# Cross attention: products over heads and keys packed into five chunks of 128 rows instead of eight of 77

## The chip, the core and the metric

The kernel runs on one core of a Trainium2 chip. The metric is the device time of one execution in microseconds (us). A core has TensorE (PE in the profile; PEld is its loading of stationary operands), VectorE (DVE), ScalarE (ACT), GpSimd (POOL) and SyncE (SP), each with its own queue of instructions in program order, and 16 DMA engines that they share. Matmuls read on-chip memory (SBUF, 128 rows called partitions) and write PSUM, from which DVE and ACT copy.

## The reference

Sixteen batches, each with 256 queries of width 256 and 77 keys of context width 192; eight heads of width 256; all float32.

```python
Q = (img_embed @ Wq).reshape(B, -1, H, D).transpose(0, 2, 1, 3)
K = (sent_embed @ Wk).reshape(B, -1, H, D).transpose(0, 2, 1, 3)
V = (sent_embed @ Wv).reshape(B, -1, H, D).transpose(0, 2, 1, 3)
score = jnp.einsum('bhqd,bhkd->bhqk', Q, K) / math.sqrt(D)
score = jnp.where(mask, score, -jnp.inf)
attn = jax.nn.softmax(score, axis=-1)
ctx = jnp.einsum('bhqk,bhkd->bqhd', attn, V).reshape(B, -1, H * D)
out = ctx @ Wo + img_embed
mu = jnp.mean(out, axis=-1, keepdims=True)
var = jnp.var(out, axis=-1, keepdims=True)
return (out - mu) * jax.lax.rsqrt(var + EPS) * gamma + beta
```

## The kernel before

The products are taken in another order. Once, for each head: G = Wq Wk^T / sqrt(D) (matmuls `pg`, kept transposed in `gT`) and U = Wv Wo (`pu`, kept in `u`); the context is transposed into `cT`, whose 192 rows lie in two chunks of 96. The weights, context and mask are loaded into a pool that is released after this stage; later tiles, `a` first of all, take its memory.

The rest is done in four groups of four batches. A batch has two tiles of 128 queries, so there are eight tiles (numbered `t`) in a group and 32 in all.

- `prepare_group`, at the first tile of a group: x is transposed (`px`, copied to `xT`) and A = G c^T is formed for the four batches and eight heads: 16 outputs `pa` of two matmuls of 308 columns, copied in turn by ACT and DVE into `a`.
- `scores_and_softmax(t)`: four matmuls of 308 columns give the scores `ps` (128 queries by 8 x 77). DVE adds the mask's bias (`s`), takes the largest of each head (`top`), subtracts it; ACT takes exp (`e`); DVE sums (`den`) and inverts (`rden`); POOL multiplies (`p`).
- `prepare_batch(b)`: the product of context and U, `pv`, with the 77 keys as output rows and 8 x 256 columns: four outputs of two matmuls of 512 columns, each copied by ACT into `vw`.
- `attend(t)`, two tiles later: eight transposes of `p`, one a head (`pp`), two ACT copies to `pT`, eight matmuls that contract 77 rows each and add up in `po` (256 columns); DVE adds the residual into `xg` and takes mean and variance (`bn`, `mv`).
- `normalise_group(g)`, after a group's last `attend`: the normalisation in two DVE steps a tile (the first one, with `gam`, is issued as soon as a tile's mean is there), then one store for two tiles.

The loop calls these with the attention product two tiles behind the scores. A scheduler orders each engine's queue from that code, so pieces of neighbouring tiles interleave; nothing overtakes within an engine's queue. The pools hold two buffers each for the scores, for transposes (`ps_tr`) and for all other products (`ps_mm`).

Of the kernel before, what the change touches and what calls it, by code (L numbers as in the profile page):

```python
# [8 lines left out]
F32 = mybir.dt.float32  # L9
# [6 lines left out]
P = 128  # L16
H = 8          # heads
D = 256        # head width
EPS = 1e-05
GB = 4         # batches in a group  # L20
MASKED = 3.0e38  # taken from a masked score: any score of less than 1e31 is absorbed by it


# Per head h the products are taken in this order:
#   G_h = Wq_h Wk_h^T / sqrt(D)        U_h = Wv_h Wo_h        (once)
#   A_bh = G_h c_b^T                   VW_bh = c_b U_h        (once a batch)
#   score_bh = x_b A_bh                out_b = sum_h softmax(score_bh) VW_bh
# so neither Q, K, V nor the context of a head is ever formed.
@with_exitstack
def kernel(  # L30
# [23 lines left out]
    HK = H // 2 * S2           # score columns in one PSUM bank  # L54
    assert NCR * CR == B * S2 and NG * GB == B and DI == 2 * P and D == 2 * P

# [14 lines left out]
    bias = const.tile([P, B, S2], F32, tag="bias", name="bias")  # L71
    live = const.tile([P, B], F32, tag="live", name="live")
    gam = const.tile([P, DI], F32, tag="gam", name="gam")
    bet = const.tile([P, DI], F32, tag="bet", name="bet")
# [7 lines left out]
    def load_x(g):  # L82
        xg = xp.tile([P, GT, DI], F32, tag="xg", name=f"xg_{g}")
        nc.sync.dma_start(xg, x_rows[:, g * GT : (g + 1) * GT, :])
        xg_of[g] = xg

    evacs = [0]

# [6 lines left out]

# [1 line left out]
    with tc.tile_pool(name="wload", bufs=1) as wp, tc.tile_pool(name="wt", bufs=2) as wt:  # L97
# [53 lines left out]
        for r in range(0, NCR, 2):  # L151
# [9 lines left out]
            for lc in range(2):  # L161
# [3 lines left out]
                )  # L165

        for h in range(H):
            wvT = transposed(wv_sb, LP, h, "wvT")
            pu = ps_mm.tile([P, 2, DI], F32, tag="mm", name=f"pu_{h}")
            for lc in range(2):  # L170
                for dc in range(2):
                    nc.tensor.matmul(  # L172
                        pu[:LP, lc, :],
                        wvT[:, dc, lc * LP : (lc + 1) * LP],
                        wo_sb[:, 2 * h + dc, :],
                        start=(dc == 0),
                        stop=(dc == 1),
                    )
            evacuate(u[:, :, h, :], pu[:LP])
# [3 lines left out]
        bias_f = bias.rearrange("p b k -> p (b k)")  # L183
# [6 lines left out]

# [1 line left out]
    ap = ctx.enter_context(tc.tile_pool(name="ap", bufs=2))  # L192
# [35 lines left out]

    def prepare_batch(b):
        vw = ap.tile([S2, H, DI], F32, tag="vw", name=f"vw_{b}", bufs=3)  # L230
        for n in range(H // 2):
            pv = ps_mm.tile([P, 2 * DI], F32, tag="mm", name=f"pv_{b}_{n}")
            for lc in range(2):
                nc.tensor.matmul(  # L234
                    pv[:S2],
                    cT[:, lc, b * S2 : (b + 1) * S2],
                    u[:, lc, 2 * n : 2 * n + 2, :].rearrange("p h d -> p (h d)"),
                    start=(lc == 0),
                    stop=(lc == 1),
                )  # L240
            nc.scalar.copy(vw[:, 2 * n : 2 * n + 2, :].rearrange("p h d -> p (h d)"), pv[:S2])  # L241
        vw_of[b] = vw

    def scores_and_softmax(t):
# [3 lines left out]
        for hh in range(2):  # L248
# [26 lines left out]
        nc.vector.tensor_scalar(rden, rden, live[:, b : b + 1], None, ALU.mult)  # L275
        p = sp.tile([P, H, S2], F32, tag="p", name=f"p_{t}")
        nc.gpsimd.tensor_tensor(  # L277
            p, e, rden.unsqueeze(2).to_broadcast([P, H, S2]), ALU.mult
        )
        p_of[t] = p  # L280

    def attend(t):
        g, b, j = t // GT, t // QT, t % GT
        p = p_of.pop(t)
        pT = sp.tile([S2, H, P], F32, tag="pT", name=f"pT_{t}", bufs=2)
        for hh in range(2):
            pt = ps_tr.tile([P, 4, P], F32, tag="tr", name=f"pp_{t}_{hh}")
            for i in range(4):
                nc.tensor.transpose(pt[:S2, i, :], p[:, hh * 4 + i, :], ident)  # L289
            nc.scalar.copy(pT[:, hh * 4 : hh * 4 + 4, :], pt[:S2])  # L290
        po = ps_mm.tile([P, DI], F32, tag="mm", name=f"po_{t}")
        for h in range(H):
            nc.tensor.matmul(  # L293
                po, pT[:, h, :], vw_of[b][:, h, :], start=(h == 0), stop=(h == H - 1)
            )
        y = xg_of[g][:, j, :]
# [71 lines left out]
```

## Time and profile before

| | |
|---|---|
| median of three runs | 482.4 us (482.24 to 482.61) |
| span of the profiled execution | 480.1 us; the page gives no other time of that execution |
| busy: PE, DVE, ACT, POOL | 439.0, 210.7, 136.8, 39.6 us |
| granted TensorE clock, mean | 0.977 |
| until the first score product is done | 98.69 us |
| the two middle groups | 98.2 us each |

The span is time from the first to the last instruction. Stretches below are cut where the first score product of a group ends, since everything before it in a group (px, pa, ps) is PE work on which all engines wait. A group line of the profile gives the source line, engine, operation and tile, the shape, the count, busy time and the mean of one in ns, then the idle time before them and what ended it. A float32 matmul appears as two records, a transpose as one.

### The profile page before, as it was taken

To read this page: it belongs to the slowest core of one execution; us is meant where nothing else is said; L and a number is where in the kernel's file an instruction comes from. 1 tells how busy PE (TensorE), PEld (TensorE's weight loads), DVE (VectorE), ACT (ScalarE), POOL (GpSimd) and SP (SyncE) were. 2 spreads that over 40 slices of the span, in tenths; PEclk is the share of its full clock that TensorE was granted. 3 is DMA by queue.
4 is the path that set the end of the run, shared out by engine and by line. 5 is a ranking of instruction groups with operands and counts; after the bars stand their busy time and mean duration, and the time that the engine had idled before them with its cause. 6 is when DMAs were issued, how large, how long until landed. Compare 5 with 4: busy or idle time off the path is not lost.

```text
span 480.1 us, 4689 instructions
## 1 busy us (share of the span) xinstructions
PE 439.0 (91%) x1846; PEld 298.3 (62%) x1846; DVE 210.7 (44%) x424; ACT 136.8 (28%) x242; POOL 39.6 (8%) x38
## 2 busy tenths in 40 slices
PE   1409899999999999999999999999999999999993
PEld 1307677755765875758567766585767756658572
DVE  0031223235736433375373433844735238555364
ACT  1103422223132222251333213523132134331321
POOL 0000000012112000121111101112111011121110
PEclk9859999999999999999999999999999999999997
DMA  8993000000000000022000000130000000200002
GB/s 237 256 341 106 0 1 1 0 2 0 0 1 0 1 0 0 1 87 89 0 0 1 0 0 2 53 123 0 1 1 0 1 0 1 89 0 0 2 1 87
DMA packets 13446, 17.86 MB, mean 37 GB/s; under 512 B 480, under 2 KB 12208, under 8 KB 13232
## 3 DMA queue, kind: packets, MB, share of 16 engines
q1 hardware_dynamic: 9696, 12.95, 8.9%
q10 hardware_dynamic: 3728, 4.62, 3.3%
q8 instruction: 14, 0.23, 0.2%
q14 instruction: 8, 0.07, 0.0%
HBM read 13.37 MB, written 4.19 MB: 37 GB/s over the span
## 4 chain that ended last, share of the span: by engine, by line
PE 87%; DMA 6%; DVE 3%; ACT 2%; issue 0%; DVEq 0%; ACTq 0%
PE po L293 24%; PE pv L234 22%; PE pa L218 14%; PE ps L250 14%; PE pp L289 5%; DMA m_i<-in_mask_BxS_if_dram 5%; PE pg L142 3%; PE pu L172 3%; DMA wk_sb<-in_L_xattn_Wk_dram 2%; PE px L205 2%; DVE wkT L94 1%; ACT pT L290 1%; DVE xg L313 1%; PE p_wkT L126 0%; PE p_wvT L126 0%
## 5 line engine op out<-in xcount | busy, mean ns | idle before, releaser
L293 PE MATMUL po<-vw,pT 77*128 77x256 f32 x512 | 117.2, 382 | 1.7 <-ACT pT L290 1.7
L234 PE MATMUL pv<-u,cT 96*77 96x512 f32 x256 | 113.1, 593 | 0.1
L293 PEld LDWEIGHTS po<-vw,pT 77*128 77x128 f32 x512 | 94.6, 190 | 21.3 <-ACT pT L290 9.7
L234 PEld LDWEIGHTS pv<-u,cT 96*77 96x77 f32 x256 | 37.5, 148 | 67.0 <-issue 57.8
L250 PE MATMUL ps<-a,xT 128*128 128x308 f32 x256 | 75.8, 422 | 0.0
L277 POOL TENSOR_TENSOR p<-e,rden 128x616 f32<-128x616 f32 x32 | 38.9, 1216 | 423.1 <-DVE rden L275 236.5
L218 PE MATMUL pa<-cT,gT 96*128 96x308 f32 x256 | 67.7, 422 | 0.0
L241 ACT COPY vw<-pv 77x512 f32<-77x512 f32 x64 | 37.1, 581 | 97.8 <-PE pv L234 97.5
L297 DVE TENSOR_TENSOR xg<-po,xg 128x256 f32<-128x256 f32 x32 | 13.6, 424 | 108.8 <-PE po L293 108.7
L290 ACT COPY pT<-pp 77x512 f32<-77x512 f32 x64 | 34.1, 583 | 86.5 <-PE pp L289 86.5
L218 PEld LDWEIGHTS pa<-cT,gT 96*128 96x128 f32 x256 | 48.0, 190 | 16.6
L250 PEld LDWEIGHTS ps<-a,xT 128*128 128x128 f32 x256 | 46.5, 190 | 12.4 <-issue 0.5
L289 PEld LDWEIGHTS pp<-ident,p 128*77 128x77 f32 x256 | 30.4, 148 | 11.3 <-issue 5.3
L94 DVE COPY a<-pa 128x308 f32<-128x308 f32 x32 | 15.3, 479 | 48.1 <-PE pa L218 48.1
L272 DVE TENSOR_REDUCE den<-e 128x8 f32<-128x616 f32 x32 | 25.4, 794 | 23.5 <-ACT e L270 23.4
L142 PE MATMUL pg<-wqT,wkT 128*96 128x256 f32 x64 | 18.9, 447 | 18.2 <-DVE wkT L94 18.2
L289 PE MATMUL pp<-ident,p 128*77 128x128 f32 x256 | 33.2, 272 | 0.0
L258 DVE TENSOR_TENSOR s<-ps,bias 128x616 f32<-128x616 f32 x32 | 25.6, 799 | 10.7 <-PE ps L250 10.7
L270 ACT ACTIVATE e<-s 128x616 f32<-128x616 f32 x32 | 22.9, 717 | 23.5 <-DVE s L266 23.4
L92 ACT COPY a<-pa 128x308 f32<-128x308 f32 x32 | 13.4, 418 | 48.3 <-PE pa L218 48.3
L142 PEld LDWEIGHTS pg<-wqT,wkT 128*96 128x96 f32 x64 | 11.6, 192 | 23.5 <-DVE wkT L94 19.8
L266 DVE TENSOR_TENSOR s<-s,top 128x616 f32<-128x616 f32 x32 | 25.6, 800 | 1.0
(45 smaller groups left out, 212.8 us busy)
## 6 DMA issues: line engine op xcount, KB each, us to landing
xg<-in_x_dram SPq DMA_DIRECT2D x4, 1024.0 KB, 12.5
out_dram<-xg SPq DMA_DIRECT2D x16, 256.0 KB, 2.2
wq_sb<-in_L_xattn_Wq_dram SPq DMA_DIRECT2D x2, 1024.0 KB, 12.3
wo_sb<-in_L_xattn_Wo_dram ACTq DMA_DIRECT2D x1, 2048.0 KB, 39.0
wk_sb<-in_L_xattn_Wk_dram ACTq DMA_DIRECT2D x2, 768.0 KB, 11.3
wv_sb<-in_L_xattn_Wv_dram SPq DMA_DIRECT2D x1, 1536.0 KB, 22.1
c_sb<-in_ctx_dram ACTq DMA_DIRECT2D x1, 924.0 KB, 27.3
m_i<-in_mask_BxS_if_dram SPq DMA_DIRECT2D x1, 616.0 KB, 21.7
```

The lines of the kernel that those rows point to most:

```text
L142: nc.tensor.matmul(pg[:LP, lc, :], wkT[:, dc, lc * LP : (lc + 1) * LP], wqT[:, dc, :], start=(dc == 0), stop=(dc == 1),)
L218: nc.tensor.matmul(pa.rearrange("p b k -> p (b k)"), gT[:, lc, h, dc * P : (dc + 1) * P], cT[:, lc, g * GB * S2 : (g + 1) * GB * S2], star ...
L234: nc.tensor.matmul(pv[:S2], cT[:, lc, b * S2 : (b + 1) * S2], u[:, lc, 2 * n : 2 * n + 2, :].rearrange("p h d -> p (h d)"), start=(lc == 0 ...
L241: nc.scalar.copy(vw[:, 2 * n : 2 * n + 2, :].rearrange("p h d -> p (h d)"), pv[:S2])
L250: nc.tensor.matmul(ps[:, hh, :HK], xT_of[g][:, dc, j * P : (j + 1) * P], a_of[g][:, dc, bl, hh * 4 : hh * 4 + 4, :].rearrange("p h k -> p ...
L258: nc.vector.tensor_tensor(s.rearrange("p (a h) k -> p a h k", a=2), ps[:, :, :HK].rearrange("p a (h k) -> p a h k", k=S2), bias[:, b, :].u ...
L266: nc.vector.tensor_tensor(s, s, top.unsqueeze(2).to_broadcast([P, H, S2]), ALU.subtract)
L272: nc.vector.tensor_reduce(den, e, AX.X, ALU.add)
L277: nc.gpsimd.tensor_tensor(p, e, rden.unsqueeze(2).to_broadcast([P, H, S2]), ALU.mult)
L289: nc.tensor.transpose(pt[:S2, i, :], p[:, hh * 4 + i, :], ident)
L290: nc.scalar.copy(pT[:, hh * 4 : hh * 4 + 4, :], pt[:S2])
L293: nc.tensor.matmul(po, pT[:, h, :], vw_of[b][:, h, :], start=(h == 0), stop=(h == H - 1))
```

## The change

The rows that the last product contracts, 8 heads x 77 keys = 616, are laid out as four chunks of 128 rows (two heads with 64 keys each) and one chunk of 104 rows (the last 13 keys of all eight heads), in place of eight chunks of 77.

- `p` is written by POOL in two parts in that order, and transposed in five pieces; the fifth, `pq`, has its own PSUM tile and its own ACT copy.
- `prepare_pair` takes the place of `prepare_batch`: one product for two batches, with 2 x 64 keys as the 128 output rows. Each output is copied in four pieces of 64 rows by 256 columns, to the rows where the packed layout wants them; ACT copies the even outputs, DVE the odd ones.
- The last 13 keys are done once for all batches, before the groups: two stages of eight batches, `pr` with 104 output rows, copied to `stage`, written to DRAM (`scratch`) by eight DMAs of 104 KB a stage, and loaded back by one DMA of 832 KB as `vr`, with (head, key) as rows.
- `cM` and `cR` are copies of `cT`, made by POOL, with the first 64 and last 13 keys of the batches side by side.

```diff
+        for lc in range(2):
+            keys = cT[:, lc, :].rearrange("p (b k) -> p b k", k=S2)
+            nc.gpsimd.tensor_copy(cM[:, lc], keys[:, :, :KM])
+            nc.gpsimd.tensor_copy(cR[:, lc], keys[:, :, KM:])
...
+        for r in range(B // RB):
+            stage = wp.tile([RB * KR, H, DI], F32, tag=("c", "wq")[r], name=f"stage_{r}")
+            for n in range(H // 2):
+                pv = ps_mm.tile([P, 2 * DI], F32, tag="mm", name=f"pr_{r}_{n}")
...
+                evacuate(
...
+            for i in range(RB):
+                nc.sync.dma_start(
+                    scratch[r * RB + i].rearrange("h k d -> k h d"),
+                    stage[i * KR : (i + 1) * KR],
+                )
+            nc.sync.dma_start(
+                vr[:, r * RB : (r + 1) * RB, :],
+                scratch[r * RB : (r + 1) * RB].rearrange("b h k d -> (h k) b d"),
+            )
...
-                    pv[:S2],
-                    cT[:, lc, b * S2 : (b + 1) * S2],
+                    pv.rearrange("p h d -> p (h d)"),
+                    cM[:, lc, b : b + 2, :].rearrange("p b k -> p (b k)"),
...
-            nc.scalar.copy(vw[:, 2 * n : 2 * n + 2, :].rearrange("p h d -> p (h d)"), pv[:S2])
-        vw_of[b] = vw
+            copy = nc.vector.tensor_copy if n % 2 else nc.scalar.copy
+            for i in range(2):
+                for half in range(2):
+                    copy(
+                        vw[i][half * KM : (half + 1) * KM, n, :],
+                        pv[i * KM : (i + 1) * KM, half, :],
+                    )
+        vw_of[b], vw_of[b + 1] = vw
...
-        for h in range(H):
-            nc.tensor.matmul(
-                po, pT[:, h, :], vw_of[b][:, h, :], start=(h == 0), stop=(h == H - 1)
-            )
+        for n in range(NF):
+            nc.tensor.matmul(po, pT[:, n, :], vw_of[b][:, n, :], start=(n == 0), stop=False)
+        nc.tensor.matmul(po, pT[:RR, NF, :], vr[:, b, :], start=False, stop=True)
...
-            if t % QT == 0:
-                prepare_batch(t // QT)
+            if t % (2 * QT) == 0:
+                prepare_pair(t // QT)
```

Three places show what becomes of the queues. A row is the source line, the operation, output and inputs, the output's shape, and how many follow each other; the number behind a tile's name is the tile or batch, and the one after it only tells buffers apart.

PE, from the first score product of the second group (tile 8), before:

```order
L250 MATMUL ps_8_989<-a_1_923,xT_1_898 128x308 x4
L234 MATMUL pv_4_0_1009<-u_78,cT_79 77x512 x2
L234 MATMUL pv_4_1_1013<-u_78,cT_79 77x512 x2
L234 MATMUL pv_4_2_1017<-u_78,cT_79 77x512 x2
L234 MATMUL pv_4_3_1021<-u_78,cT_79 77x512 x2
L289 MATMUL pp_6_0_1026<-ident_70,p_6_808 77x128 x4
L289 MATMUL pp_6_1_1032<-ident_70,p_6_808 77x128 x4
L250 MATMUL ps_9_1051<-a_1_923,xT_1_898 128x308
L293 MATMUL po_6_1038<-vw_3_810,pT_6_1025 128x256 x8
```

The same place now:

```order
L304 MATMUL ps_8_1015<-a_1_949,xT_1_924 128x308 x4
L282 MATMUL pv_4_0_1037<-u_78,cM_88 128x512 x2
L282 MATMUL pv_4_1_1044<-u_78,cM_88 128x512 x2
L347 MATMUL pp_6_1066<-ident_70,p_6_861 128x128 x2
L282 MATMUL pv_4_2_1051<-u_78,cM_88 128x512 x2
L347 MATMUL pp_6_1066<-ident_70,p_6_861 128x128 x2
L350 MATMUL pq_6_1072<-ident_70,p_6_861 104x128
L304 MATMUL ps_9_1085<-a_1_949,xT_1_924 128x308
L282 MATMUL pv_4_3_1058<-u_78,cM_88 128x512 x2
L354 MATMUL po_6_1075<-vw_3_755,pT_6_1065 128x256 x4
L355 MATMUL po_6_1075<-vr_82,pT_6_1065 128x256
```

The four pv outputs no longer follow each other: the third waits for ACT's copies of the first, the fourth for DVE's copies of the second, and the scheduler has put transposes and a score matmul between them.

DVE at the same place, before:

```order
L258 TENSOR_TENSOR s_8_994<-ps_8_989,bias_80 128x616
L265 TENSOR_REDUCE top_8_996<-s_8_994 128x8
L266 TENSOR_TENSOR s_8_994<-s_8_994,top_8_996 128x616
L272 TENSOR_REDUCE den_8_1001<-e_8_999 128x8
L274 RECIPROCAL rden_8_1003<-den_8_1001 128x8
L275 TENSOR_SCALAR rden_8_1003<-rden_8_1003,live_81 128x8
L297 TENSOR_TENSOR xg_0_103<-po_6_1038,xg_0_103 128x256
```

And now:

```order
L312 TENSOR_TENSOR s_8_1020<-ps_8_1015,bias_80 128x616
L319 TENSOR_REDUCE top_8_1022<-s_8_1020 128x8
L320 TENSOR_TENSOR s_8_1020<-s_8_1020,top_8_1022 128x616
L326 TENSOR_REDUCE den_8_1027<-e_8_1025 128x8
L292 COPY vw_4_1035<-pv_4_1_1044 64x256
L328 RECIPROCAL rden_8_1029<-den_8_1027 128x8
L292 COPY vw_4_1035<-pv_4_1_1044 64x256
L329 TENSOR_SCALAR rden_8_1029<-rden_8_1029,live_81 128x8
L292 COPY vw_5_1036<-pv_4_1_1044 64x256 x2
L292 COPY vw_4_1035<-pv_4_3_1058 64x256 x2
L292 COPY vw_5_1036<-pv_4_3_1058 64x256 x2
L357 TENSOR_TENSOR xg_0_109<-po_6_1075,xg_0_109 128x256
```

Eight copies stand between tile 8's softmax and the end of tile 6; those of pv_4_1, for which PE's fourth output waits, stand behind `den`, which waits for ACT's exp. The group's second pair adds eight more.

SP, between the last load of the first stage and the first store, now (with what each waits for; before, nothing stood here):

```order
L93 DMA xg_1_114<-in_x_dram 128x8x256 [waits DMAHW3_49]
L218 DMA scratch_87<-stage_0_424 13x8x256 [waits DMAHW4_49,DVE_49,Activation_49]
...
L218 DMA scratch_87<-stage_0_424 13x8x256 [waits DMAHW3_49]
L218 DMA scratch_87<-stage_1_450 13x8x256 [waits DMAHW4_49,DVE_49,Activation_49]
L222 DMA vr_82<-scratch_87 104x8x256 [waits DMAHW5_49,DMAHW3_49,DMAHW6_49,DMAHW2_49,DMAHW7_49,DMAHW1_49,DMAHW0_49]
L218 DMA scratch_87<-stage_1_450 13x8x256 x6
L218 DMA scratch_87<-stage_1_450 13x8x256 [waits DMAHW4_49]
L222 DMA vr_82<-scratch_87 104x8x256 [waits DMAHW4_49,DMAHW5_49,DMAHW3_49,DMAHW6_49,DMAHW2_49,DMAHW7_49,DMAHW1_49,DMAHW0_49]
```

Eighteen transfers were added. ACT's and DVE's first copies into `a` of the first group, which takes the memory of the released pool, wait until all sixteen writes from `stage` are done; they don't wait for `vr`.

More of the change, by code (lines that the diff above doesn't have):

```diff
@@ L20 @@
 GB = 4
+KM = 64
 MASKED = 3.0e38
@@ L54 @@
     HK = H // 2 * S2
+    NF = H // 2
+    KR = S2 - KM
+    RR = H * KR
+    RB = 8
     assert NCR * CR == B * S2 and NG * GB == B and DI == 2 * P and D == 2 * P
@@ L72 @@
     live = const.tile([P, B], F32, tag="live", name="live")
+    vr = const.tile([RR, B, DI], F32, tag="vr", name="vr")
     gam = const.tile([P, DI], F32, tag="gam", name="gam")
@@ L85, in load_x @@
         xg_of[g] = xg
+    dram = ctx.enter_context(tc.tile_pool(name="dram", bufs=1, space=bass.MemoryType.DRAM))
+    scratch = dram.tile([B, H, KR, DI], F32, tag="scratch", name="scratch")
+    cM = const.tile([LP, 2, B, KM], F32, tag="cM", name="cM")
+    cR = const.tile([LP, 2, B, KR], F32, tag="cR", name="cR")
     evacs = [0]
@@ L275, in scores_and_softmax @@
         nc.vector.tensor_scalar(rden, rden, live[:, b : b + 1], None, ALU.mult)
-        p = sp.tile([P, H, S2], F32, tag="p", name=f"p_{t}")
-        nc.gpsimd.tensor_tensor(
-            p, e, rden.unsqueeze(2).to_broadcast([P, H, S2]), ALU.mult
-        )
+        p = sp.tile([P, H * S2], F32, tag="p", name=f"p_{t}")
+        for cols, keys in ((slice(NF * P), slice(KM)), (slice(NF * P, None), slice(KM, None))):
+            part = p[:, cols].rearrange("p (h k) -> p h k", h=H)
+            nc.gpsimd.tensor_tensor(
+                part,
+                e[:, :, keys],
+                rden.unsqueeze(2).to_broadcast(list(part.shape)),
+                ALU.mult,
+            )
         p_of[t] = p
@@ L284, in attend @@
         p = p_of.pop(t)
[L285 to L290, printed above, removed]
+        pT = sp.tile([P, NF + 1, P], F32, tag="pT", name=f"pT_{t}", bufs=2)
+        pt = ps_tr.tile([P, NF, P], F32, tag="tr", name=f"pp_{t}")
+        for n in range(NF):
+            nc.tensor.transpose(pt[:, n, :], p[:, n * P : (n + 1) * P], ident)
+        nc.scalar.copy(pT[:, :NF, :], pt)
+        pt = ps_tr.tile([P, NF, P], F32, tag="tr", name=f"pq_{t}")
+        nc.tensor.transpose(pt[:RR, 0, :], p[:, NF * P :], ident)
+        nc.scalar.copy(pT[:RR, NF, :], pt[:RR, 0, :])
         po = ps_mm.tile([P, DI], F32, tag="mm", name=f"po_{t}")
-        for h in range(H):
-            nc.tensor.matmul(
-                po, pT[:, h, :], vw_of[b][:, h, :], start=(h == 0), stop=(h == H - 1)
-            )
+        for n in range(NF):
+            nc.tensor.matmul(po, pT[:, n, :], vw_of[b][:, n, :], start=(n == 0), stop=False)
+        nc.tensor.matmul(po, pT[:RR, NF, :], vr[:, b, :], start=False, stop=True)
         y = xg_of[g][:, j, :]
```

18 lines of the change are left out of this document (14 added, 4 removed).

## The prediction

> **What bounds the kernel now.** I read the page first: busy shares, the 40 slices, the chain that ended last.
>
> ```profile
> span 480.1 us, 4689 instructions
> PE 439.0 (91%) x1846; PEld 298.3 (62%) x1846; DVE 210.7 (44%) x424; ACT 136.8 (28%) x242; POOL 39.6 (8%) x38
> PE   1409899999999999999999999999999999999993
> PEclk9859999999999999999999999999999999999997
> PE 87%; DMA 6%; DVE 3%; ACT 2%; issue 0%; DVEq 0%; ACTq 0%
> ```
>
> TensorE (PE) is full from the fourth slice to the last, at the full granted clock, and 87% of the chain is its work. Next I cut the span where the first score product of each group ends (98.69, 187.95, 286.15, 384.36 us). Columns: length, busy time of PE, PEld, DVE, ACT, POOL with counts, clock, DMA.
>
> ```profile
> 98.69:187.95 89.26, 88.97 (x354) 58.26 (x352) 42.32 (x82) 25.57 (x46) 9.73 (x8) 1.00 0.00 0
> 286.15:384.36 98.21, 97.92 (x401) 65.76 (x400) 48.78 (x99) 30.49 (x53) 9.73 (x8) 1.00 0.07 22
> 384.36:480.10 95.74, 86.57 (x360) 57.96 (x358) 50.33 (x106) 29.66 (x49) 9.73 (x8) 0.97 0.07 23
> ```
>
> In the steady group PE idles 0.3 us of 98.2, so every us off PE is a us off the time until another engine ends last. VectorE (DVE) is next with 48.8 us. The price of PE's work comes from the chain in order of time, where pieces stand end to end (a float32 matmul is two records):
>
> ```profile
> 149.17 6.87 PE pv L234 x16
> 157.44 3.49 PE po L293 x16
> 80.55 16.07 PE pa L218 x62
> 96.62 2.07 PE ps L250 x8
> ...
> 234.33 1.04 PE L289 MATMUL pp<-ident,p 128*77 128x128 f32 x8
> 235.21 0.68 PE L250 MATMUL ps<-a,xT 128*128 128x308 f32 x2
> ```
>
> A pv matmul of 512 columns costs 6.87/8 = 0.859 us, a po matmul of 256 columns 3.49/8 = 0.436, a pa or ps matmul of 308 columns 0.519 each. 308 columns cost the same with 96 rows contracted (pa) as with 128 (ps), so I take rows and output rows as free: packing costs nothing on PE. Eight transposes take 235.21-234.33 = 0.88 us, 0.11 each.
>
> **What the change takes off PE.** Per pair of batches pv falls from 16 matmuls to 8, per tile po from 8 to 5 and the transposes from 8 to 5. In one group: 16 x 0.859 = 13.7, 24 x 0.436 = 10.5, 24 x 0.11 = 2.6, together 26.8 us. Over the kernel that is 64 x 0.859 + 96 x 0.436 + 96 x 0.11 = 107.4 us. The new products pr add 16 x 0.859 = 13.7 us once. Net PE 93.7 us less.
>
> **What it adds at the start.** The copies into cM and cR on POOL (2464 columns at p's 1.22 us for 616, 4.9 us) run while PE forms U, four times the 3.69 us below; of POOL's 38 instructions 32 are in the groups, so it is free, and without that cover they would cost their 4.9. The rows on the way through DRAM, and on U's end (74.54 + 3.69 = 78.2):
>
> ```profile
> out_dram<-xg SPq DMA_DIRECT2D x16, 256.0 KB, 2.2
> m_i<-in_mask_BxS_if_dram SPq DMA_DIRECT2D x1, 616.0 KB, 21.7
> 211.01 2.75 SPq L318 DMA_DIRECT2D out_dram<-xg  x4
> 212.00:215.00 3.00, 3.00 (x10) 1.07 (x9) 2.50 (x7) 1.55 (x4) 0.20 (x1) 1.00 1.01 335
> wo_sb<-in_L_xattn_Wo_dram ACTq DMA_DIRECT2D x1, 2048.0 KB, 39.0
> ...
> 74.54 3.69 PE pu L172 x16
> ...
> 35.13 3.48 PE L142 MATMUL pg<-wqT,wkT 128*96 128x256 f32 x8 [16.86 <-DVE wkT L94]
> 39.60 1.97 PE L142 MATMUL pg<-wqT,wkT 128*96 128x256 f32 x8 [0.21 <-DVE wkT L94]
> ```
>
> The first copy into `a` waits until the second staging tile has been read out, because `a` lies in its memory; the half load of vr stands ahead of seven of its eight writes in SP's queue. pr ends at 78.2 + 13.7 = 91.9, its last eviction 0.9 later (0.68 and a hop of 0.2) at 92.8; nine issues at about 0.5 us (2.75/4 = 0.69 is the upper row) 97.3; landing 2.2: 99.5. By bytes, 1.6 MB at 335 GB/s is 4.7 us behind about 95. I take 101, and 101.7 for the buffer's release. PE has 16 transposes and two pa outputs to do meanwhile (3.8 us, until 95.7), then waits 6 us, and restarts slower: after its wait of 16.86 us eight pg records took 3.48 instead of 1.97, so +1.5. Fourteen pa outputs (14.5) and ps (2.1) put the end of the first score product at 119.8, not 98.7. Bounds: no wait 112; a landing like m_i's, 21.7 us, 133. vr itself is needed only by the first po, some 14 us later, and is covered. Nothing else queues behind on SP until the first output.
>
> **What it adds on DVE, and why I don't book the whole 26.8.** One tile's DVE work in the steady part, in order of time:
>
> ```profile
> 239.42 0.42 DVE L297 TENSOR_TENSOR xg<-po,xg 128x256 f32<-128x256 f32 x1 [7.08 <-PE po L293]
> 239.88 0.43 DVE L299 BATCH_NORM_STATS2 bn<-xg 128x6 f32<-128x256 f32 x1
> 240.34 0.18 DVE L300 BATCH_NORM_AGGREGATE mv<-bn 128x2 f32<-128x6 f32 x1
> 240.56 0.48 DVE L310 SCALAR_TENSOR_TENSOR xg<-xg,mv,gam 128x256 f32<-128x256 f32 x1
> 240.98 0.80 DVE L258 TENSOR_TENSOR s<-ps,bias 128x616 f32<-128x616 f32 x1
> 241.81 0.80 DVE L265 TENSOR_REDUCE top<-s 128x8 f32<-128x616 f32 x1
> 242.64 0.80 DVE L266 TENSOR_TENSOR s<-s,top 128x616 f32<-128x616 f32 x1
> 244.28 0.79 DVE L272 TENSOR_REDUCE den<-e 128x8 f32<-128x616 f32 x1 [0.84 <-ACT e L270]
> 245.18 0.20 DVE L274 RECIPROCAL rden<-den 128x8 f32<-128x8 f32 x1
> 245.42 0.23 DVE L275 TENSOR_SCALAR rden<-rden,live 128x8 f32<-128x8 f32 x1
> ...
> 471.95 0.42 DVE L297 TENSOR_TENSOR xg<-po,xg 128x256 f32<-128x256 f32 x1 [3.26 <-PE po L293]
> ...
> 473.73 3.26 DVE L313 SCALAR_TENSOR_TENSOR xg<-xg,rstd,bet 128x256 f32<-128x256 f32 x8
> ...
> L94 DVE COPY a<-pa 128x308 f32<-128x308 f32 x32 | 15.3, 479 | 48.1 <-PE pa L218 48.1
> L94 DVE COPY xT<-px 128x512 f32<-128x512 f32 x8 | 5.4, 679 | 2.0 <-PE px L205 2.0
> L241 ACT COPY vw<-pv 77x512 f32<-77x512 f32 x64 | 37.1, 581 | 97.8 <-PE pv L234 97.5
> ```
>
> A tile takes 6.2 us on DVE, 0.84 of it waiting for exp. The change gives DVE 16 copies of 256 columns a group. Between 308 columns at 479 ns and 512 at 679 a column costs about 1 ns, so one is 0.43 us (bounds 0.33, in proportion to columns, and 0.69, no cheaper than a 512 one; I take the line, as the form is the same). ACT's 16 cost 0.29 to 0.58 by its row of 512; even at 0.58 ACT has no more of them than now, and with the 8 small copies of pT (under 0.58 each) in place of 8 large ones it has room in 30.5 of 98.2 us.
>
> During the 18 us of px and pa DVE can only keep step with PE. The softmax of eight tiles and eight tile ends must fit in the other stretch, where PE now has only 98.2-26.8-18.4 = 53.0 us of work (18.4: pa 16.07 + 0.52, 16 transposes 1.8). DVE's rows from s of a group's first tile to the first xT copy of the next, in the order of the changed program: 8 x 3.19 (s, top, sub, den) = 25.5; 7 x 0.43 (rden twice) = 3.0; 8 x 1.03 (y, bn, mv) = 8.3; 7 x 0.48 = 3.4; 16 x 0.43 = 6.9; rstd and L313 3.5; xT 0.7: 51.3. With 103 gaps of 0.04 (s ends 241.78, top starts 241.81) 4.1. Waits: exp has DVE work behind it in the queue for four of the eight tiles; for the others 4 x 0.84 = 3.4. And a new one: pv_4_3 on PE waits until DVE has copied pv_4_1, which stands behind s, top, sub and den (4.3 us after ps ends) and takes four copies with two small rows between (2.3), so that PE starts it about 7 us after ps; DVE then sits 2.3 us until it ends and 0.6 more until po. Sum 61.7. POOL's two parts of p stay near 9.73/8 = 1.22 us and off this path.
>
> A group is then 0.2 (hop) + 61.7 + 0.2 + 0.4 (px) + 29 x 0.519 = 15.1 (the rest of pa) + 2.1 (ps) = 79.7 us: 18.5 saved, 8.3 of 26.8 given back. The same sum for the first group (six tile ends, three bare exps, two waits of 2.2 for pv) is 55.4 on DVE, 73.4 in all. In the last, DVE's rows to the final rden (62.2) are followed by p, transposes, copy and po (5.5) and today's tail of 8.2 (480.1-471.95): 76.1.
>
> Sum: 119.8 + 73.4 + 2 x 79.7 + 76.1 = 428.7 us of span against 480.1. The median of the runs, 482.4, is 2.3 above the span; with the same 2.3 the prediction is 431 us.
>
> The Trainium skill, TensorEngine Tiling (Array Packing), section Performance Considerations, PSUM Bottleneck, warns that a faster TensorE leaves PSUM copying as the limit and advises sharing it between ScalarE and VectorE. By that rule the sum is 431; by PE's rows alone it would be 396. This trace cannot show it, since PE is full here, and by my rows it is DVE's share of the copies that makes the difference.
>
> **Rivals.**
> PE stays the bound: the waits overlap and nothing but pr and the start (7.5) comes back: 480.1-93.7+7.5+2.3 = 396. For it: DVE's 51.3 plus gaps 4.1 is near PE's 53.0. Against: the queue is in order, and the pv wait sits in it.
> DVE costs more: all eight exps bare (+3.4) and the second pair's pv wait as long as the first (+2.3), in four groups +23: 454. For it: today every den has its 0.84 wait. Against: in the changed order other rows stand there.
> The way through DRAM is slow: 21.7 us landing, 444. Break-even needs 51 us more than I book, above even wo's 39.0.
> Slower than before, by the clock: PE's gaps let the granted clock fall. pg at the low clock cost 3.48/1.97 = 1.77 times. PE's 371 us after the first score product become 264; the 51 us that I book are eaten when 51/0.77 = 67 us of that run cold, a quarter. Against: a wait of 16.86 us did it, the next of 0.21 us did not; my longest wait in the loop, for DVE's xT copy, is about 3 us. All of it cold gives 431 + 0.77 x 264 = 634. The Trainium skill, TensorE: Matmul & The Clock Gate, Part 1 on the HAM clock gate, puts the drop to half clock at an idle window of about 3.4 us; by that rule the start wait goes cold and the loop stays warm, near its edge, and the trace agrees with the first (3.48).
>
> **Chances.** Forecast (414 to 446) 0.60; PE bound or nearly (393 to 414) 0.17; DVE costs more, or the slow DRAM way (446 to 470) 0.18; 470 to the time before 0.02; clock, slower than before, 0.03. The range, 406 to 455, leaves out about 0.08 below and 0.12 above. Faster by over 0.2% 0.96, within 0.2% (about what the runs, 482.24 to 482.61, can tell from no change) 0.01, slower 0.03.
>
> **What would show it.** Windows between the score products near 73, 80, 80, 76 us; PE busy near 345 us; copies on DVE near 430 ns; PE waiting for DVE at pv and px, and once about 6 us for pa; DVE busy over 80% outside pa. Wrong if PE stays at 99% in the groups, if the clock row falls below 9, or if the first score product ends far from 120.

## The result and the profile after

The changed kernel takes 413.2 us (412.5 to 414.4, four runs) against 482.3; ratio 0.856, 95% interval 0.853 to 0.858. The forecast was 431 with a range of 406 to 455, so the time lies inside it, 18 us below the point. The profiled execution is the slowest of the four, 414.4 us with a span of 412.4.

The page of the changed kernel, the rows that stood first before:

```profile
span 412.4 us, 4082 instructions
PE 352.2 (85%) x1462; PEld 245.6 (60%) x1462; DVE 228.2 (55%) x492; ACT 115.0 (28%) x246; POOL 50.3 (12%) x74
PE   0604989994799999999999999999999999999972
PEclk9955999998599999999999999999999999999997
PE 47%; DVE 32%; DMA 9%; ACT 7%; issue 3%; SPq 1%; ACTq 0%; DVEq 0%
```

PE's row has a new dip in the tenth and eleventh slices (4 and 7, with the clock at 8 and 5), and from there to the tail it reads 9. The chain now names DVE for 32% of the span. That looks like a second bound; the windows say otherwise. Cut as before, where each group's first score product ends (columns: length, busy time of PE, PEld, DVE, ACT, POOL with counts, clock, DMA share, GB/s):

```profile
126.28:195.51 69.23, 66.52 (x267) 45.82 (x267) 46.95 (x98) 20.33 (x46) 11.57 (x16) 1.00 0.00 0
269.49:343.46 73.97, 71.71 (x297) 50.77 (x297) 52.19 (x115) 24.39 (x53) 11.80 (x16) 1.00 0.09 29
343.46:412.40 68.94, 57.13 (x238) 40.07 (x237) 53.60 (x122) 23.04 (x49) 11.81 (x16) 0.96 0.09 31
```

A middle group takes 74.0 us, of which PE works 71.7 and DVE 52.2. PE idles 2.3 us where it idled 0.3. What it waits for there, from the waits of PE in this window (us in total, times, longest):

```profile
PE pv L282 <- ACT vw L292: 0.9, 2, 0.6
PE px L251 <- ACT xT L106: 0.7, 1, 0.7
PE po L354 <- ACT pT L348: 0.6, 1, 0.6
```

All three are hand-overs from ACT, none from DVE directly. DVE stands behind one of them: the longer wait at pv, 0.61 us, ends at 300.09 with copies that ACT does behind an exp, and that exp waited until 297.93 for DVE's subtraction. Still, all of PE's idle time is 2.3 us of 74.0, so by this profile no other engine can have cost more than that in a group. Against the forecast:

| | predicted | measured |
|---|---|---|
| first score product done | 119.8 | 126.3 |
| first group | 73.4 | 69.2 |
| each middle group | 79.7 | 74.0 |
| last group and tail | 76.1 | 68.9 |
| span | 428.7 | 412.4 |

From the first score product to the end it was 381.4 us (480.1 - 98.69) and is 286.1. PE lost 107.4 us of work there by the sum of the prediction, and 95.3 of it arrived: 12 us were given back in four groups, where the forecast booked 35. Of the 12, PE's idle time grew by 9.0 (by 2.4, 2.0, 2.0 and 2.6 in the four groups); the other 3 are busy time, which fell by 104.3 and not by 107.4. The start went the other way, 6.5 us worse than forecast. (Some of that varies: in the seven other traces with this start, the first score product is done between 124.4 and 126.8.) There, in order of time on PE, then the DMA issues on SP's queue, then the one piece of the chain between them:

```profile
95.83 1.72 PE L264 MATMUL pa<-cT,gT 96*128 96x308 f32 x6
106.11 18.10 PE L264 MATMUL pa<-cT,gT 96*128 96x308 f32 x56 [8.55 <-ACT a L106]
```

```profile
87.62 7.15 SPq L218 DMA_DIRECT2D scratch<-stage  x9
95.02 0.30 SPq L222 DMA_DIRECT2D vr<-scratch  x1
95.37 5.58 SPq L218 DMA_DIRECT2D scratch<-stage  x7
```

```profile
100.05 5.25 DMA scratch<-stage
```

PE stands still for 8.55 us until ACT may copy into `a`, and ACT waits for the last write of the staging tiles: issued at 100.0, landed at 105.3. After that 56 records of pa take 18.1 us. The windows around the wait show why (the column before the last two is the granted clock):

```profile
95.90:97.50 1.60, 1.60 (x7) 0.89 (x6) 0.69 (x1) 0.24 (x1) 0.00 (x0) 1.00 0.62 76
97.60:99.40 1.80, 0.00 (x0) 0.00 (x0) 0.00 (x0) 0.00 (x0) 0.00 (x0) 0.94 0.74 194
99.60:106.10 6.50, 0.00 (x0) 0.00 (x0) 0.38 (x1) 0.42 (x1) 0.00 (x0) 0.50 0.65 175
106.20:112.20 6.00, 6.00 (x12) 4.02 (x13) 0.48 (x1) 0.42 (x1) 0.00 (x0) 0.50 0.69 145
113.00:124.00 11.00, 11.00 (x44) 8.07 (x43) 2.40 (x5) 2.17 (x6) 0.00 (x0) 1.00 0.01 1
```

The clock is halved within 2 us of PE's last matmul and stays halved for 6 us of full work after the restart.

### The profile page after: what moved, and what is told of

Its sections match the earlier page's. It is cut to its first block, busy times and chain, and to the rows that moved or that the text cites. A ratio compares the mean times of both kernels' runs of the same rounds, so it can differ in the third digit from the quotient of the medians.

```text
span 412.4 us, 4082 instructions
## 1 busy us (share of the span) xinstructions
PE 352.2 (85%) x1462; PEld 245.6 (60%) x1462; DVE 228.2 (55%) x492; ACT 115.0 (28%) x246; POOL 50.3 (12%) x74
## 4 chain that ended last, share of the span: by engine, by line
PE 47%; DVE 32%; DMA 9%; ACT 7%; issue 3%; SPq 1%; ACTq 0%; DVEq 0%
PE pa L264 16%; PE pv L282 9%; DMA m_i<-in_mask_BxS_if_dram 5%; DVE s L320 5%; DVE top L319 4%; DVE s L312 4%; PE po L354 4%; ACT e L324 4%; PE pg L156 4%; DVE xg L370 4%; PE pu L191 4%; PE ps L304 3%; DVE den L326 3%; PE pr L206 3%; DVE xg L373 3%
## 5 line engine op out<-in xcount | busy, mean ns | idle before, releaser
L333 POOL TENSOR_TENSOR p<-e,rden 128x512 f32<-128x512 f32 x64 | 47.0, 755 | 289.6 <-DVE rden L329 156.3
L354 PE MATMUL po<-vw,pT 128*128 128x256 f32 x256 | 61.1, 381 | 4.7 <-ACT pT L348 4.7
L282 PE MATMUL pv<-u,cM 96*128 96x512 f32 x128 | 60.0, 602 | 3.9 <-ACT vw L292 2.7
L354 PEld LDWEIGHTS po<-vw,pT 128*128 128x128 f32 x256 | 48.1, 190 | 17.2 <-ACT pT L348 7.6
L304 PEld LDWEIGHTS ps<-a,xT 128*128 128x128 f32 x256 | 46.5, 190 | 13.4 <-issue 1.4
L282 PEld LDWEIGHTS pv<-u,cM 96*128 96x128 f32 x128 | 23.0, 189 | 31.4 <-issue 19.8
L324 ACT ACTIVATE e<-s 128x616 f32<-128x616 f32 x32 | 22.9, 716 | 55.6 <-DVE s L320 55.6
L292 DVE COPY vw<-pv 64x256 f32<-64x256 f32 x64 | 26.9, 421 | 15.1 <-PE pv L282 14.1
L348 ACT COPY pT<-pp 128x512 f32<-128x512 f32 x32 | 18.6, 583 | 56.4 <-PE pp L347 56.2
L326 DVE TENSOR_REDUCE den<-e 128x8 f32<-128x616 f32 x32 | 25.3, 791 | 14.8 <-ACT e L324 14.6
L292 ACT COPY vw<-pv 64x256 f32<-64x256 f32 x64 | 23.4, 365 | 29.4 <-PE pv L282 28.5
L319 DVE TENSOR_REDUCE top<-s 128x8 f32<-128x616 f32 x32 | 25.1, 783 | 0.3
L347 PEld LDWEIGHTS pp<-ident,p 128*128 128x128 f32 x128 | 16.0, 141 | 10.5 <-issue 5.3
```

Of the source, the lines that this page charges most:

```text
L282: nc.tensor.matmul(pv.rearrange("p h d -> p (h d)"), cM[:, lc, b : b + 2, :].rearrange("p b k -> p (b k)"), u[:, lc, 2 * n : 2 * n + 2, :] ...
L292: copy(vw[i][half * KM : (half + 1) * KM, n, :], pv[i * KM : (i + 1) * KM, half, :],)
L304: nc.tensor.matmul(ps[:, hh, :HK], xT_of[g][:, dc, j * P : (j + 1) * P], a_of[g][:, dc, bl, hh * 4 : hh * 4 + 4, :].rearrange("p h k -> p ...
L319: nc.vector.tensor_reduce(top, s, AX.X, ALU.max)
L324: nc.scalar.activation(e, s, AF.Exp)
L326: nc.vector.tensor_reduce(den, e, AX.X, ALU.add)
```

## The experiments

Two theories for the groups. **P**: PE's work still sets the length of a group. **D**, the prediction's: DVE's queue does, between one group's first `s` and the next group's first copy of xT. That stretch is 55.6 us now (269.52 to 325.12), and PE has 53.0 of work beside it, so D in its measured size would also explain the 2.3 us of idle PE: the traces alone do not tell them apart. In question is what those 2.3 us are, and which engine's work would have to change for a group to change. For the start: the wait is the memory that `a` shares with the staging tiles, and the slow pa is the clock. Times below are medians; 413.2 is the changed kernel.

**own_memory.** The staging tiles lie where `a` does not.

```diff
-            stage = wp.tile([RB * KR, H, DI], F32, tag=("c", "wq")[r], name=f"stage_{r}")
+            stage = sgp.tile([RB * KR, H, DI], F32, tag="stage", name=f"stage_{r}")
```

`sgp` is a pool of its own, opened after the pool of wq, wk and c is released; `a`, which then lies over wv and wo, and `vw` are put in separate pools.

> The two staging tiles get a pool of their own, in memory that the first group's `a` does not take; the writes to DRAM and the loads of vr stay as they are. In the changed kernel (413.2 us) PE waited 8.55 us for the first copies into `a`, and its 56 records of pa took 18.1 us where they took 14.5 before, with the granted clock at 0.50 for 6.5 us after the restart. Theory (the wait is the memory shared with the staging tiles, and the cold clock follows from the wait): both go, 12.2 us, about 401. Rival A (only the wait goes, pa is slow for another reason): about 404.7. Rival B (the first attention product then waits for vr, which lands some 5 us after the last write): most of it comes back, 408 to 413.

400.9 us, ratio 0.830 (0.829 to 0.832). PE:

```profile
95.46 16.23 PE L271 MATMUL pa<-cT,gT 96*128 96x308 f32 x62
```

The wait and the slow records are both gone, 12.3 us in all, as the theory had it. vr still travels as before and delays nothing.

**warm_wait.** The wait stays, PE is kept busy in it.

```diff
+                if g == 0 and h == 0 and dc == 1:
+                    for _ in range(2):
+                        pz = ps_sc.tile([P, 2, 512], F32, tag="sc", name=f"pz_{_}")
+                        for i in range(32):
+                            nc.tensor.transpose(pz[:, 0, :P], xT[:, 1, (GT - 1) * P :], ident)
```

> The wait for `a` stays, but PE is given 64 transposes of no use in it, behind the second pa output (about 0.11 us each, 7.0 us). Theory (pa after the wait is slow because the clock fell in the wait): the granted clock stays at 1.00, pa's 56 records take 14.5 us again instead of 18.1, so 3.6 us less than the changed kernel: about 409.6. Rival (pa is slow because ACT and DVE have to catch up on their copies): no change, 413, or up to 1 us more if the transposes outlast the wait.

411.1 us, ratio 0.852 (0.851 to 0.854); its interval just touches the changed kernel's, so the rows carry the verdict:

```profile
96.95 7.15 PE L276 MATMUL pz<-ident,xT 128*128 128x128 f32 x64
106.67 14.78 PE L264 MATMUL pa<-cT,gT 96*128 96x308 f32 x56 [2.57 <-ACT a L106]
```

The same 56 records take 14.8 us in place of 18.1, with the same copies in front; the granted clock is 1.00 from 106.7 to 112.7. The slow pa was the clock, 3.3 us of it; ACT and DVE had nothing to catch up. The time fell by 2.1 where 3.6 was expected: pa restarts 0.56 us later here (106.67 for 106.11), and the profiled spans differ by 2.7 (409.7 and 412.4).

**unpaired.** pv for one batch at a time, as two sets of matmuls with 64 output rows.

```diff
+            for i in range(2):
+                for lc in range(2):
+                    nc.tensor.matmul(
+                        pv[i * KM : (i + 1) * KM].rearrange("p h d -> p (h d)"),
+                        cM[:, lc, b + i, :],
...
```

> pv is formed for one batch at a time again (64 output rows, two sets of matmuls into the two halves of the same PSUM tile); copies, layout and everything else as in the changed kernel. It adds 64 matmuls of 512 columns at 0.859 us, 55.0 us of PE work, 13.7 a group. Theory P (PE's work sets the length of a group, the 2.3 us that it idles are small losses of hand-over): plus 13.7 a group, about 468. Theory D (as predicted, DVE's queue sets it, with a stretch of 55.6 us beside PE's 53.0 of work): PE's stretch has to pass DVE's first, so plus 11.1 a group, about 457. If output rows were not free (half of them at half the price), it would stay near 413.

416.9 us, ratio 0.864 (0.863 to 0.866): 3.7 us more, neither theory's number but that of the last sentence. One pv output in this kernel, eight records, and then one in the changed kernel, four:

```profile
201.96 1.94 PE L283 MATMUL pv<-u,cM 96*64 96x512 f32 x8
```

```profile
202.12 1.88 PE L282 MATMUL pv<-u,cM 96*128 96x512 f32 x4
```

Twice the matmuls take the same time. So this kernel added hardly any PE work and says nothing on P and D. It asked for two more, `pv_twice` and `halves`.

**halves.** Three stretches of 12 matmuls of 512 columns behind the changed kernel's last work: 128 output rows, 64 rows in the lower half, 64 rows in both halves in turn.

```diff
+    for k, halves in enumerate(((0, 0), (0, 0), (0, 1))):
+        m = KM if k else P
...
+            lo = halves[i % 2] * KM
+            nc.tensor.matmul(
+                pz[lo : lo + m, :],
...
```

> Behind the changed kernel's last work come three stretches of 12 matmuls of 512 columns, 96 rows contracted: 128 output rows; 64 output rows, always the lower half; 64 output rows, lower and upper half in turn. In `unpaired`, matmuls of 64 output rows cost about half. Theory A (a matmul of 64 output rows is cheaper by itself: its two records run side by side): the second and third stretch both have a pitch of about 0.43 to 0.5 us against 0.86. Theory B (matmuls of different halves run beside each other): only the third stretch is fast, the second has 0.86. The time itself tells nothing but some 25 us more at the end.

```profile
408.95 13.67 PE L406 MATMUL pz<-z,cM 96*128 96x512 f32 x24 [5.53 <-DVE z L399]
423.85 10.51 PE L406 MATMUL pz<-z,cM 96*64 96x512 f32 x24 [1.23 <-DVE z L414]
435.68 5.37 PE L406 MATMUL pz<-z,cM 96*64 96x512 f32 x24 [1.32 <-DVE z L414]
```

(The first stretch begins at the half clock after a wait.) In one half, 12 matmuls of 64 rows take 10.51 us, 0.88 each, nearly the 0.86 of 128 rows. In alternate halves they take 5.37. Theory B: matmuls of different halves run beside each other. Two things stay open. Matmuls of one half here also write the same PSUM rows each time, so this run does not separate the half of the array from the rows that are written. And in `unpaired` the code issues both products of the lower half before those of the upper, yet its records also start in pairs; the trace does not name the half of a record, so how they came to stand in turn is not shown. The Trainium skill, TensorEngine Tiling (Array Packing), Overview, promises up to two times for a stationary side of at most 64 columns by splitting the array into independent tiles; the trace agrees, 10.51 against 5.37, and shows that it takes both halves.

**pv_twice.** More PE work that can't hide so: each pv output computed twice over.

```diff
-            for lc in range(2):
+            for lc in (0, 1, 0, 1):
```

> Each pv output is computed twice over, into the same rows, so that the matmuls can't stand beside each other in the array; all else as in the changed kernel (413.2 us). It adds 64 matmuls of 512 columns at 0.859 us, 13.7 us of PE work in each group of 74.0 with 71.7 of PE work now. Theory P (PE's work sets a group): plus 13.7 a group, 55 in all, about 468; a little less where the second pass covers a wait that PE has at pv now, so 459 to 470. Theory D (DVE's queue sets it, PE's stretch of 53.0 first has to pass DVE's 55.6): plus 11.1 a group, about 457 or below.

461.9 us, ratio 0.956 (0.954 to 0.959), 48.7 more. A middle group:

```profile
292.97:379.07 86.10, 84.74 (x329) 57.03 (x329) 52.28 (x115) 24.57 (x53) 11.80 (x16) 1.00 0.08 25
```

12.1 us more a group. PE's busy time rose by 13.0, not by the full 13.7, and 0.9 of it went into PE's idle time, which fell from 2.3 to 1.4 (its waits for pv are gone). It is P's number, though D's 11.1 is not far, so this run alone does not settle it.

**copies_act.** No copies of vw on DVE.

```diff
-            copy = nc.vector.tensor_copy if n % 2 else nc.scalar.copy
+            copy = nc.scalar.copy
```

> All copies of vw on ACT, none on DVE: 16 copies of 0.42 us a group leave DVE's queue, and with them its waits for pv. Theory D (DVE's queue sets the groups): its stretch falls from 55.6 to about 46, below PE's 53.0, so a group gains the 2.3 us that PE idles: about 404. Theory P (PE sets them): nothing to gain, 410 to 413. Rival (ACT's queue, with exp and the copies of pT between, now delays pv's buffers): slower, 413 to 425.

416.1 us, ratio 0.862 (0.861 to 0.863): 2.8 slower.

```profile
268.66:343.75 75.09, 72.25 (x298) 50.68 (x297) 46.08 (x99) 30.32 (x69) 11.80 (x16) 1.00 0.09 29
```

DVE has 6.1 us less to do in a group, and the group is 1.1 longer. D's 404 did not come. But the time lies in the range of the third outcome, ACT's queue delaying pv's buffers, so this run does not exclude a gain on DVE that ACT took back. Of the 1.1 us, 0.6 is idle time of PE, in which its waits for ACT grow from 2.2 to 2.6 us (pv 0.9, po 0.9, px 0.8), and 0.5 is busy time of PE; why that grew is not known.

**copies_twice.** Each copy on DVE issued twice.

```diff
-                    copy(
+                    for _ in range(1 + n % 2):
+                        copy(
```

> Every copy of vw that stands on DVE is issued twice: 16 more copies of 0.42 us a group, 6.9 us of DVE work, 27 us in all; PE's work is unchanged. Theory D (DVE's queue sets a group): all of it comes back, about 441. Theory P (PE sets it, DVE has 22 of 74 us to spare): most of it disappears in DVE's idle time, and what is left is the hand-over, since the fourth pv output waits 1.75 us longer for the copies of the second, twice a group: 413 to 427.

422.6 us, ratio 0.874 (0.872 to 0.877): 9.4 more, of 27 us of added work.

```profile
271.21:347.10 75.89, 72.69 (x297) 50.59 (x297) 58.69 (x131) 24.57 (x53) 12.50 (x16) 1.00 0.08 29
```

6.5 us more DVE work in this group, and the group is 1.9 longer. DVE's idle time takes the rest, as P has it; D's 441 is far off.

**no_last_product.** The other side: less PE work, the same on DVE.

```diff
-        nc.tensor.transpose(pt[:RR, 0, :], p[:, NF * P :], ident)
-        nc.scalar.copy(pT[:RR, NF, :], pt[:RR, 0, :])
...
-        nc.tensor.matmul(po, pT[:RR, NF, :], vr[:, b, :], start=False, stop=True)
```

> The transpose pq, its ACT copy and the fifth product of each tile are left out, so the last 13 keys don't enter the output; they are still formed at the start. PE loses 32 times 0.4325 + 0.11 = 0.54 us, 17.4 us in all, 4.3 in each middle group; DVE's work is unchanged. Theory P (PE's work sets a group, also from below): each middle group falls by most of 4.3, to 70 to 71, and the whole by 13 to 17, to 396 to 400. Theory D (DVE's queue sets it): DVE's stretch stays at 55.6, the groups at 74.0, and only the end of the last group gains 0.9: about 412. Between them, about 406, if DVE's queue becomes the bound after some 2 us a group.

396.7 us, ratio 0.822 (0.819 to 0.825): 16.5 less of the 17.4.

```profile
261.56:330.73 69.17, 67.98 (x273) 46.64 (x273) 51.38 (x115) 22.98 (x45) 12.01 (x16) 1.00 0.09 31
```

A group falls by 4.8 us, with DVE's instructions as they were. This settles it: DVE's stretch is no fixed length. It was 55.6 us because PE gave it that long; here it is 50.5 (from `s` at 261.59 to the first xT copy's end at 312.11):

```profile
261.59 0.80 DVE L312 TENSOR_TENSOR s<-ps,bias 128x616 f32<-128x616 f32 x1 [1.60 <-PE ps L304]
...
311.43 0.68 DVE L108 COPY xT<-px 128x512 f32<-128x512 f32 x1
```

Of the 4.8, 3.7 left PE's busy time and 1.1 its idle time, which fell from 2.3 to 1.2; the ACT copy that went too may be behind the latter. P holds, and D is out.

**dve_neighbours.** Why DVE's queue was shorter than its sum. Behind the last work, 12 copies in a chain and 12 from one source.

```diff
+    for i in range(12):
+        nc.vector.tensor_copy(z[(i + 1) % 2][:, :DI], z[i % 2][:, :DI])
+    for i in range(12):
+        nc.vector.tensor_copy(z[1 + i % 2][:, (i // 2 % 2) * DI : (i // 2 % 2 + 1) * DI], z[0][:, :DI])
```

> Behind the changed kernel's last work DVE copies 256 columns by 128 rows 12 times in a chain, each reading what the one before wrote, and then 12 times from one source to four places in turn, none reading what another wrote. Theory (the prediction's 0.04 us between neighbours holds only where an instruction waits for the one before it; else it starts about 0.1 us before the recorded end): starts in the chain are one duration plus 0.03 to 0.04 us apart, in the other row one duration less 0.07 to 0.10 us. Rival (the early starts in the groups come from the kind of the instructions or from PSUM operands): both rows have the same pitch. The time itself tells nothing but some 8 us more of DVE work at the end.

DVE in order of time, and the groups with their mean of one:

```profile
408.99 3.90 DVE L400 COPY z<-z 128x256 f32<-128x256 f32 x12
412.93 2.51 DVE L402 COPY z<-z 128x256 f32<-128x256 f32 x12
```

```profile
L400 DVE COPY z<-z 128x256 f32<-128x256 f32 x12 | 3.5, 294 | 0.5
L402 DVE COPY z<-z 128x256 f32<-128x256 f32 x12 | 2.5, 287 | 0.0
```

Starts in the chain are (3.90 - 0.29)/11 = 0.328 us apart, 0.034 more than one takes; in the other row (2.51 - 0.29)/11 = 0.202, 0.085 less. As the theory had it.

**own_memory_early_mask.** own_memory, and the mask loaded ahead.

```diff
             nc.scalar.dma_start(wk_sb[:, :, cols], wk_r[:, :, cols])
+            if i == 0:
+                nc.sync.dma_start(m_i, mask.rearrange("b k -> (b k)").partition_broadcast(P))
```

> own_memory, and the mask's load is issued behind the first halves of the key and query weights, not behind all the weights and x. In the changed kernel as before it, PE waits 17.9 us near the start for a copy of wkT, which stands in DVE's queue behind the bias, and that waits for the mask until 32.5 us. Theory: the mask lands at about 15, the wait goes but for some 3.5 us of mask work on DVE, and all later work moves forward by about 14.5: 386 against own_memory's 400.9. Rival (the start is bound by the transfer of 10 MB of weights, which lasts until 41 us): PE waits for wv or wo later, and about half comes back: 393. Rival (the mask's 616 KB take 20 us also ahead): no change, 401.

387.5 us, ratio 0.802 (0.800 to 0.804). First PE in the changed kernel, then here:

```profile
36.28 3.73 PE L156 MATMUL pg<-wqT,wkT 128*96 128x256 f32 x8 [17.91 <-DVE wkT L108]
```

```profile
18.09 1.11 PE L143 MATMUL p_wqT<-ident,wq_sb 128*128 128x128 f32 x4 [6.10 <-DVE wkT L108]
```

13.4 us of the 14.5 expected: the mask's work on DVE begins at 14.36 us, not 32.55, and one wait of 6.1 us is left. The weights' transfer was not the bound.

**tail_in_two.** The same, with the last group's second normalisation step in two parts.

```diff
+            if d == NT - 3:
+                normalise_group(NG - 1, 0, GT - 2)
+            if d == NT - 1:
+                normalise_group(NG - 1, GT - 2, GT)
```

> own_memory_early_mask (387.5), and the last group's second normalisation step is done for its first six tiles while the last two tiles' products run, and for those two at the end. After the last residual DVE then has 2 of these steps instead of 8 of 0.40 us pitch: 2.4 us less, about 385.1, if ACT's change from exp to square root, which now stands before the last copy of pT, is covered. Rival: the change of table delays that copy and the end by about 1.3 us: 386.4.

384.9 us, ratio 0.797 (0.794 to 0.799), the fastest kernel here: 2.6 less than the one before it, so the change of ACT's table is covered. The last row of DVE is now two steps, where the changed kernel has eight:

```profile
378.96 0.88 DVE L381 SCALAR_TENSOR_TENSOR xg<-xg,rstd,bet 128x256 f32<-128x256 f32 x2
```

```profile
406.13 3.26 DVE L373 SCALAR_TENSOR_TENSOR xg<-xg,rstd,bet 128x256 f32<-128x256 f32 x8
```

## Where the prediction was right, and where its sum was off

**The range held, in part by luck.** The mechanism that the point of 431 rests on, DVE's queue as the bound of the groups, was wrong. The time lies just below the forecast's own bracket (414 to 446, chance 0.60) and in that of the rival in which PE stays the bound (393 to 414, chance 0.17). Two errors worked against each other: the groups and the tail were booked 22.8 us too long (308.9 for 286.1), the start 6.5 too short; without the second the time would have been at the lower end of the range, near 407. Of its own signs, the price of a copy came as it said, and so did DVE's busy share (47.07 of 55.60 us, 85%); but PE's waits for DVE at pv and px did not come in the middle group, where it waits for ACT. A high busy share did not make DVE the bound.

**PE's part was right.** The rows of a matmul are free here from 77 up to 128: po with 128 rows contracted takes 1.73 us for eight records (0.4325 a matmul, 0.436 before), pv with 128 output rows 0.86 a matmul as with 77:

```profile
276.26 1.72 PE pv L282 x4
277.98 1.73 PE po L354 x8
```

In the middle groups PE's busy time fell by 26.2 us (97.92 to 71.71) for the 26.8 of the sum.

**The step that failed is the DVE stretch of 61.7 us.** Its sizes for the new work held: a copy of 256 columns took 421 ns for the 0.43 assumed, and DVE's new wait for pv 2.16 us for 2.3:

```profile
L292 DVE COPY vw<-pv 64x256 f32<-64x256 f32 x64 | 26.9, 421 | 15.1 <-PE pv L282 14.1
```

```profile
269.52 0.80 DVE L312 TENSOR_TENSOR s<-ps,bias 128x616 f32<-128x616 f32 x1 [1.60 <-PE ps L304]
270.36 0.80 DVE L319 TENSOR_REDUCE top<-s 128x8 f32<-128x616 f32 x1
...
278.01 1.73 DVE L292 COPY vw<-pv 64x256 f32<-64x256 f32 x4 [2.16 <-PE pv L282]
...
285.04 0.80 DVE L326 TENSOR_REDUCE den<-e 128x8 f32<-128x616 f32 x1 [0.84 <-ACT e L324]
285.75 0.41 DVE L357 TENSOR_TENSOR xg<-po,xg 128x256 f32<-128x256 f32 x1
286.08 0.19 DVE L328 RECIPROCAL rden<-den 128x8 f32<-128x8 f32 x1
```

Two things were wrong. The first is the term of 103 gaps of 0.04, booked as 4.1 us. `top` needs `s` and starts 0.04 after its end; the residual's sum (xg) does not need `den` and starts 0.09 before its end (285.04 + 0.80 = 285.84, start 285.75). In the old queue neighbours mostly depended on each other, in the new one they mostly come from different tiles, and dve_neighbours gives the two prices, +0.034 and -0.085. Counted in the trace, 66 of the 103 steps in this stretch start before the recorded end of the one ahead (18 of 85 in the same stretch before), together 5.4 us early; the small gaps of the others come to 0.8. So the term was -4.6 us, not +4.1. The window has 47.07 us of DVE busy, where the rows and gaps came to 55.4:

```profile
269.52:325.12 55.60, 53.34 (x224) 37.16 (x222) 47.07 (x104) 20.80 (x45) 10.43 (x14) 1.00 0.12 38
```

That term alone makes the overshoot: with it as measured, the prediction's own sum is 51.3 - 4.6 + 6.3 (its waits) = 53.0, no more than PE's work beside it. The rows (52.6 for 51.3) and the waits (7.7 for 6.3) came out longer than booked.

The second is an error in kind, not in size: I added the waits to the stretch as if they were DVE's own. The other 8.5 us of the window are nearly all waits for PE and ACT, and they shrink and grow with PE: in no_last_product 5.2 us of the stretch are left of them (50.52 less 45.28 of work), and in pv_twice the waits for pv alone are 11.9 us in a group, for 3.3 here. With 47.1 of work DVE had room in the stretch, and PE's 53 us set its length. So the first rival (PE stays the bound, waits overlap) was the true mechanism, though its 396 was too low: it took PE's rows at their full price with no more idle time than before, where 12 us were given back (9 of them idle), and it took the start as forecast. 396 + 12 + 6.5 is 414.5 against 414.4, but both additions are read from this same run, so that is book-keeping and no test.

The last group follows from the same stretch: its 62.2 us of DVE rows to the final rden were 55.7 (343.46 to 399.2). What follows took 13.2 us for the 13.7 of the sum.

**The start was under-sized by 6.5 us**, 6.0 of them in three terms. pr began at 79.8 us and not at 78.2, with the same PE work ahead of it; 1.05 of that is the first long wait for wkT, 17.91 for 16.86. The wait was 8.55 us where I had 6: the last seven issues took 5.58 us, 0.8 each where I took 0.5, and the last write landed after 5.25 us where I took 2.2, the landing of the output stores. The cold clock cost 3.3 us where I took 1.5: I priced eight records after a restart, and here 12 longer ones ran at half clock. (The bound of 133 us for a slow landing counts its 21.7 us from the last eviction; behind the nine issues it would be 138. Nothing came near it.)

**The copies out of PSUM** as the limit gave 431 in the prediction's sum, PE's rows 396. The measured 413 lies between, but the mechanism is PE's: doubling DVE's share of these copies cost 9.4 of 27 us (copies_twice). The Trainium skill, TensorEngine Tiling (Array Packing), Performance Considerations, PSUM Bottleneck, says that copying may become the limit when TensorE gets faster, and advises to use both ScalarE and VectorE. No run here shows copying as the limit; sharing was right, since ACT alone was 2.8 us slower (copies_act).

**The clock.** The granted clock was 1.00 in all groups but the one with the tail (0.96), so the rival of a cold loop did not come. At the start it fell within 2 us of the last matmul and came back after 6 to 7 us of work (between 112.2 and 113.0). In the kernel before, PE restarts at 35.13 after its wait of 16.86 us, and there the clock is back between 38 and 39, some 3 us later:

```profile
38.00:39.00 1.00, 1.00 (x9) 0.78 (x8) 0.02 (x1) 0.35 (x1) 0.00 (x0) 0.89 1.10 347
```

The Trainium skill, TensorE: Matmul & The Clock Gate, Part 1, puts the fall behind at least one idle window and the return behind at least one busy window of about 3.4 us, and says that the window runs freely. Counted from PE's stop, the fall here came sooner than that; the returns after some 3 and after 6 to 7 us do not contradict it.

## What to carry to other kernels

Before an engine with waits in its queue is added up into a bound, separate its work from its waits: the work is a floor, the waits give way to whoever is really late. A staging buffer that borrows memory from a released pool ties the next stage to its last DMA, and the idle engine may pay again for its clock; giving it memory of its own was worth 12.3 us for a few lines of pool declarations. An engine that is busy 85% of a stretch need not be its bound. And the head of a queue deserves a look before its middle: an early load of the mask gained 13.4 us that neither kernel's change had touched.

## What was unexpected in the hardware

- Matmuls with 64 output rows in different halves run beside each other: 12 in 5.37 us against 10.51 in one half (and one set of PSUM rows).
- In copies of 256 columns within SBUF, DVE starts an instruction 0.085 us before the recorded end of the one ahead unless it waits for it; then 0.034 after. The copies of vw, whose outputs start in turn at rows 0 and 64, don't gain: four take 1.73 us, 0.44 apart at 0.421 each. The Trainium skill, VectorE: DVE Perf Modes, Two Vector instructions with no wait between them, says that an instruction whose output starts in another quadrant than the last is held until all before it are done; the trace agrees with that.
- The clock fell within 2 us of PE's last matmul, and after the wait of 8.55 us it took 6 to 7 us of work to come back; before, after a wait of 16.86 us, some 3.
- Writes of 104 KB from 13 rows issued 0.8 us apart on SP, and the last, behind the half load of vr, landed after 5.25 us, against 0.69 and 2.2 for the 256 KB stores.
